# A threshold search with fewer passes, its secant steps on other engines, and logits computed in pairs of row groups

## The chip, the cores and the metric

The kernel runs on one core of one Trainium2 chip. The metric is the device time of one execution in microseconds (us), from the first to the last instruction of that core. Times quoted are medians of several executions. A profile is one more execution, taken by the hardware profiler. Below, PE is TensorE (PEld its weight loads), DVE is VectorE, ACT is ScalarE, POOL is GpSimd. The granted clock is the share of its full speed that the profile gives for PE.

## The reference, cut to what matters

```python
# x: (3327, 256); adj: (3327, 3327), some 0.24% of its entries and the diagonal not zero
h = relu(layernorm(x))
Xf = Xa = h
for n in range(2):                                  # "step 0" and "step 1" below
    q = Xa @ W1.T @ W2.T                            # (3327, 64)
    k = Xa @ W3.T
    p = softmax(q @ k.T)                            # 3327 x 3327
    # nucleus: a row's largest probabilities, kept while the sum of those before is < 0.9
    idx = argsort(-p); sp = p sorted; cs = cumsum(sp)
    mask = scatter(cs - sp < 0.9)
    A = p * mask; A = A / A.sum(-1)
    Xf = R @ Xf                                     # R: (adj + identity), rows normalised
    Xa = A @ Xa
    Z = Z + Xf @ U1[n].T + Xa @ U2[n].T
x = x + layernorm(h + Z)
out = x + relu(adj_norm @ relu(layernorm(x)) @ W.T + b)   # "the final product" below
```

The kernel doesn't sort 3327 probabilities a row. For each row it looks for a threshold on the exponentials `e` that has some 12 to 14 entries fewer above it than the true cut. It then finds the cut among the few largest entries below the threshold. A row that this misses would be found by a test at the end of the program, which takes a slow exact branch.

## The kernel before

The rows go through in 26 blocks of 128, first all of step 0, then all of step 1, then the final product. A block is cut into some hundred pieces. Each piece has a place, a time in us relative to the block's window pass. The program issues all pieces of all blocks in the order of place plus 30 us times the block's number, so several blocks overlap. The numbers set the order in which an engine takes its pieces, and only that: each engine works in order, and waits where its inputs are late.

```python
PERIOD = 30.0
PLACES = (dict(lda0=-85.27, ..., ev1r=-27.94, ev1s=-26.31, st1=-25.42, ..., few=-18.62,   # cut
               st2a=-14.35, ..., st2=-8.7, ..., win=0, ..., drop=20.87, ...),
          dict(xtq_t=-67.29, ..., st2=-16.38, nt2=-16.32, ev3=-15.89, gv1=-12.86, st3=-9.5,  # cut
               nt3=-4.48, ..., win=0, ..., drop=6.98, ...))
```

The search. `e` is 128 x 3327. A pass of ACT sums `relu(t - e)` or `sign(t - e)` over it. The mass pass of DVE sums the entries above `t`. Everything else acts on columns of 128 x 1:

```python
def fma(name, src, scale, bias, f=AF.Identity):        # one column, on ACT
    dst = col(name)
    nc.scalar.activation(dst, src, f, bias=bias, scale=scale)
    return dst

def eval_pass(s, f, name):                             # 3.07 us on ACT
    # ... (junk: a tile that nobody reads)
    nc.scalar.activation(junk, s["e"][:, :N], f, bias=s["t"], scale=-1.0, accum_out=s[name])

def not_few(s):                                        # step 0, on POOL
    nc.gpsimd.tensor_scalar(few, s["sign"], N - 2 * FEW, FAR, op0=ALU.is_lt, op1=ALU.mult)
    nc.gpsimd.tensor_tensor(few, few, s["u"], op=ALU.subtract)
    set_thr(s)

def secant(s, goal):                                   # step 1, on POOL
    t, kc, d = s["t"], s["kc"], s["up"]
    nc.gpsimd.tensor_scalar(num, d, -1.0, d, op0=ALU.mult, op1=ALU.max)
    nc.gpsimd.tensor_scalar(num, t, kc, num, op0=ALU.mult, op1=ALU.add)
    nc.gpsimd.tensor_tensor(slope, s["excess"], s["before"], op=ALU.subtract)
    # ... seven more of this kind, with one pow(den, -1)

def eval_mass(s):                                      # step 1, 3.68 us on DVE
    nc.vector.scalar_tensor_tensor(junk, ev, s["t"], ev, op0=ALU.is_gt, op1=ALU.mult, accum_out=s["mass"])

def drop_rest(i, step, s):                             # "the drop pass", 3.68 us on DVE, once a block
    nc.vector.scalar_tensor_tensor(
        ev, s.pop("w")[:, :N], kept8[:, step * NB + i, 0:1], ev, op0=ALU.is_gt, op1=ALU.mult, accum_out=den)
```

Step 0 evaluates a sum and a count at each of two thresholds, four passes of ACT. Step 1 does the same, then a secant step on POOL, a mass pass on DVE, and a second secant step on POOL.

The logits. Keys lie in two halves of 64 partitions each, so each matmul uses half of the array's rows:

```python
LOGIT_CHUNKS = []                                      # eight chunks, up to 512 columns of one half each
for _c in range(0, HC, 512):
    for _h in range(2):
        _w = min(512, (HC if _h == 0 else N - HC) - _c)
        LOGIT_CHUNKS.append((_h, _c, _w, _h * HC + _c))

def logit_chunk(s, kt, n):                             # eight separate pieces of a block
    half, c0, w, at = LOGIT_CHUNKS[n]
    s["l", n] = pl = ps_l.tile([P, 512], F32, tag="psl", name="p_l")
    rows = slice(half * DA, (half + 1) * DA)
    nc.tensor.matmul(pl[:, :w], s["q"][rows, :], kt[rows, c0 : c0 + w], start=True, stop=True)

def exp_chunk(s, n):                                   # eight exponentials, each with its sum
    nc.scalar.activation(
        s["e"][:, at : at + w], s.pop(("l", n))[:, :w], AF.Exp, accum_out=s["zp"][:, n : n + 1])
```

The product with `R` adds each block's own rows on DVE (piece `prop`) before ACT scales them. POOL issues the gathers: 16 a block in step 0 (eight rows of `adj`, eight of `h`), eight in step 1.

Of the kernel before, what the change touches and what calls it, by code (L numbers as in the profile page):

```python
# [17 lines left out]
P = 128  # L18
# [15 lines left out]
LOGIT_CHUNKS = []  # L34
for _c in range(0, HC, 512):
    for _h in range(2):
        _w = min(512, (HC if _h == 0 else N - HC) - _c)
        LOGIT_CHUNKS.append((_h, _c, _w, _h * HC + _c))
# [37 lines left out]
AIM = (14.0, 12.0)  # L76


QUANT = 1.2815516
DENS = (0.1754983, 0.1595439)  # L80
# [5 lines left out]
FEW = 20.5  # L86
FAR = 60.0
# [18 lines left out]
        lda0=-85.27, flag0=-72.55, lda1=-69.11, xtq_t=-69, lda2=-67.9, xtq_c=-66.8,  # L106
        flag1=-63.82, lda3=-62.27, q1_m=-59.1, flag2=-58.44, q1_c=-56.97, q2_m=-53.29,
        q2_c=-50.53, lg0=-49.96, ex0=-49.75, flag3=-47.66, lg7=-47.53, lg6=-45.4,
        ex7=-44.92, lg4=-44.85, ex6=-44.23, listA=-42.72, lg3=-40.26, ex4=-39.87,
        listN=-39.78, before=-39.78, lg2=-39.65, lg1=-39.48, beforec=-39.06, ex3=-38.97,  # L110
        lg5=-38.89, ex2=-38.69, ex1=-38.26, owners=-36.57, ex5=-36.04, shared=-34.28,
        guess=-33.47, lentc=-33.42, which=-30.52, ev1r=-27.94, ev1s=-26.31, st1=-25.42,
        rows=-21.78, ev2s=-20.12, few=-18.62, ev2r=-15.77, st2a=-14.35, idx=-9.35,
        gv5=-8.72, st2=-8.7, ga0=-5.98, gv3=-4.27, gv7=-1.49, gv4=-1.09, gv1=-0.73,
        win=0, wm0=2.18, wm1=3.73, wm2=6.42, ga5=7.09, gv6=7.44, wm3=9.54, gv0=9.6,
        ga1=9.71, diag=9.75, ga4=10.48, sort=13.78, cut=15.85, ga7=17.26, match=19.36,
        drop=20.87, tr0=21.98, atc0=23.34, tr1=24.39, atc1=25.24, tr2=25.35, att0=25.73,
        tr3=26.42, att1=26.62, atc2=26.87, ga2=27.32, atc3=28.01, tr4=28.07, ga6=29.35,
        gv2=29.61, ga3=30.18, att2=32.01, atc4=32.29, att3=33.26, tr6=34.12, atc6=34.36,
        tr5=35.01, inv=36.42, att4=37.74, atc5=38.12, adj0=38.16, att5=38.64, att6=39.87,  # L120
        attend=39.94, adj1=41.04, stxa=41.5, adj2=42.64, adj3=43.47, adj4=43.71,
        xtk_t=44.19, adj5=44.33, adj6=44.34, xtk_c=44.73, store=45.09, adj7=45.44,
        adj8=48.38, k_m=49.7, k_c=50.09, degA=51.5, prop=52.89, deg=55.98, scale=70.99,
        stxf=84.28,
    ),
    dict(
        xtq_t=-67.29, xtq_c=-62.17, q1_m=-62.02, q1_c=-61.59, q2_m=-58.75, q2_c=-56.62,
        lg0=-55.22, lg4=-54.87, ex0=-52.74, lg3=-51.08, ex4=-50.37, lg7=-48.98, ex3=-47.8,
        lg2=-47.44, ex7=-46.65, lg5=-46.01, ex2=-45.98, ex5=-43.9, lg1=-43.28, lg6=-42.45,
        ex1=-41.17, ex6=-40.83, guess=-38.51, ev1r=-32.26, ev1s=-31.87, st1=-27.61,  # L130
        gv6=-25.6, ev2r=-25.53, ev2s=-24.8, st2a=-24.23, gv7=-21.66, st2=-16.38,
        nt2=-16.32, ev3=-15.89, gv1=-12.86, st3=-9.5, nt3=-4.48, gv5=-4.32, gv0=-1.63,
        win=0, wm0=0.03, wm1=0.86, ld2=0.92, wm2=0.99, wm3=3.29, gv2=4.09, sort=5.17,
        cut=5.26, lda=6.33, match=6.43, drop=6.98, gv4=9.13, gv3=12.4, inv=16.86,
        tr1=18.26, tr0=20.4, atc1=21.2, tf1=21.53, tr2=21.87, tf1c=22.32, adj0=22.42,
        atc0=23.35, atc2=23.87, adj1=24.05, adj2=24.85, adj3=25.18, att0=25.2, adj4=26.4,
        adj5=26.46, tr3=26.7, att1=27.9, adj6=27.96, tr5=28.47, att2=28.91, atc3=29.97,
        adj7=31.68, tr4=32.86, adj8=33.13, atc5=33.42, atc4=33.61, tr6=33.66, prop=33.84,
        att3=33.9, att4=34.32, atc6=34.75, scale=35.17, att5=36.88, mix0=36.94, att6=36.95,
        tf2=38.31, mix1=38.9, attend=39.79, tf2c=40.97, ta2=41.25, ldx=42.46, ta2c=44.29,  # L140
        mix2=47.26, mix3=49.69, resid=50.09, root1=51.53, input2=52.12, root2=80.43,
        node2=81.03, stn=91.32,
# [21 lines left out]
def tile_kernel(ctx: ExitStack, tc: tile.TileContext, x, adj_t, w1t, w2t, w3t, u1t, u2t, ln_g, ln_b, wt, bias, out):  # L164
# [8 lines left out]
    ps_l = ctx.enter_context(tc.tile_pool(name="ps_l", bufs=3, space=bass.MemoryType.PSUM))  # L173
# [3 lines left out]
    ps_m = ctx.enter_context(tc.tile_pool(name="ps_m", bufs=1, space=bass.MemoryType.PSUM))  # L177
# [70 lines left out]

    values = [LN_EPS, 1e-9, 1e-6, -1.0, DOWN, -DOWN, FAR - 2 * DOWN, -0.5 * N, AIM[0] - 0.5 * N]
    values += [-float(np.log(N * d)) for d in DENS]  # L250
# [134 lines left out]
    def list_chunk(i, c, s):  # L385

        if c == 0:
            s["most"] = small.tile([P, NB], F32, name="most", bufs=2)
        b0, nb = ADJ_CHUNKS[c]
        nc.vector.tensor_reduce(  # L390
            s["most"][:, b0 : b0 + nb], s["chunk"].pop(c)[:, :nb, :], AX.X, ALU.max, apply_absolute_value=True
        )
# [21 lines left out]
    def list_before(s):  # L414
        s["p"] = before = ps_m.tile([P, 512], F32, tag="psm", name="p_before")
        nc.tensor.matmul(before[:, 0:1], tri, s["count"], start=True, stop=True)
# [12 lines left out]
    def list_shared(s):  # L429

        s["p"] = p_sh = ps_m.tile([P, 512], F32, tag="psm", name="p_shared")
        w = OVER + 2
        for k in range(SHARED):
            nc.tensor.matmul(
                p_sh[:, k * w : (k + 1) * w], s["own"][:, k * P : (k + 1) * P], s["nodes"][:, SHARED + REG :],
                start=True, stop=True,
            )
# [65 lines left out]
    def adj_gathered(s, k, width, own, acc=adj_acc):  # L503


        if k == 0:
            s["acc"] = acc()
        rows = own if k == SLOTS else s["vg"].pop(k)
        nc.tensor.matmul(  # L509
            s["acc"][:, :width], s["ac"][:, k, :], rows[:, :width], start=(k == 0), stop=(k == SLOTS)  # L510
        )
# [4 lines left out]
    def turn(s, src, space=(ps_m, "psm")):  # L516
# [20 lines left out]
    def key(s, xt, space=(ps_m, "psm")):  # L537
        s["p"] = pk = space[0].tile([P, 512], F32, tag=space[1], name="p_k")
# [23 lines left out]
    def centre(kt, key_sum):  # L562
# [3 lines left out]
        pm = ps_m.tile([P, 512], F32, tag="psm", name="p_mean")  # L566
# [5 lines left out]
    def query_1(s):  # L572
        s["p"] = pq1 = ps_m.tile([P, 512], F32, tag="psm", name="p_q1")
# [7 lines left out]
    def query_2(s):  # L581
        s["p"] = pq = ps_m.tile([P, 512], F32, tag="psm", name="p_q")
# [6 lines left out]
    def logit_chunk(s, kt, n):  # L589
        half, c0, w, at = LOGIT_CHUNKS[n]  # L590
        s["l", n] = pl = ps_l.tile([P, 512], F32, tag="psl", name="p_l")
        rows = slice(half * DA, (half + 1) * DA)
        nc.tensor.matmul(pl[:, :w], s["q"][rows, :], kt[rows, c0 : c0 + w], start=True, stop=True)  # L593

    def exp_chunk(s, n):

        half, c0, w, at = LOGIT_CHUNKS[n]
        if n == 0:
            s["e"] = big.tile([P, N + FILL], F32, tag="e", name="e", bufs=3)
            s["zp"] = small.tile([P, NZ], F32, name="zp")  # L600
        nc.scalar.activation(  # L601
            s["e"][:, at : at + w], s.pop(("l", n))[:, :w], AF.Exp, accum_out=s["zp"][:, n : n + 1]
# [14 lines left out]
    def first_guess(s, step):  # L617

        s["z"] = col("z")
        junk = small.tile([P, NZ], F32, name="junk_z", bufs=1)  # L620
# [7 lines left out]
        ln_c = fma("ln_c", ln_z, -1.0, value[-float(np.log(N * DENS[step]))])  # L628
        s["c"] = fma("c", ln_v, 0.5, ln_c, AF.Exp)

# [6 lines left out]
    def excess(s, aim=0.0):  # L637

        below = fma("below_n", s["sign"], -0.5, value[aim - 0.5 * N])
        rest = fma("rest", s["z"], 1.0 - TOP_P, s["over"])  # L640
        s["before"], s["excess"] = s.get("excess"), fma("excess", below, s["t"], rest)

    def density_step(s):

        s["up"] = fma("up", s["excess"], s["c"], value[DOWN], AF.Relu)

    def step_1(s):
        excess(s)
        density_step(s)
        s["u"] = fma("u1", s["up"], 1.0, s["u"])  # L650
        s["t"] = fma("t1", s["u"], 1.0, value[-DOWN], AF.Exp)

    def mark_few(s):
        s["few"] = few = col("few")
        nc.gpsimd.tensor_scalar(few, s["sign"], N - 2 * FEW, FAR, op0=ALU.is_ge, op1=ALU.mult)

    def not_few(s):
        s["few"] = few = col("few")
        nc.gpsimd.tensor_scalar(few, s["sign"], N - 2 * FEW, FAR, op0=ALU.is_lt, op1=ALU.mult)
        nc.gpsimd.tensor_tensor(few, few, s["u"], op=ALU.subtract)  # L660
        set_thr(s)
# [4 lines left out]

    def step_2(s):

        s["u"] = fma("u2", s["up"], -1.0, s["few"], AF.Relu)
        s["t"] = fma("t2", s["u"], -1.0, value[FAR - 2 * DOWN], AF.Exp)  # L670

    def secant(s, goal):

        num, den, slope, up, u = (col(n) for n in ("num", "den", "slope", "up_s", "u_s"))
        t, kc, d = s["t"], s["kc"], s["up"]
        nc.gpsimd.tensor_scalar(num, d, -1.0, d, op0=ALU.mult, op1=ALU.max)  # L676
        nc.gpsimd.tensor_scalar(num, t, kc, num, op0=ALU.mult, op1=ALU.add)
# [662 lines left out]
```

## Time and profile before

| | before |
|---|---|
| median of 3 runs | 2070.38 us (2068.54 to 2074.57) |
| span of the profiled execution | 2153.0 us, mean granted PE clock 0.919 |
| a block of step 0 / of step 1, by the stretches in the prediction | 29.25 / 35.5 us |
| ACT passes of 3.07 us a block, step 0 / step 1 | 4 / 4 (and one mass pass on DVE in step 1) |

The profile's page gives the chain of work that ended last, by engine, and below that its costliest groups of instructions. A row of a group has line, engine, operation, the tiles written and read, their shapes and the count; then busy us and mean ns; then idle time just ahead of it and what ended it. Of the kernel before:

```profile
PE 38%; ACT 34%; POOL 16%; issue 8%; DVE 2%; DMA 1%; another core or an unknown queue 1%; POOLq 0%; SPq 0%; ACTq 0%; DVEq 0%
...
L593 PE MATMUL p_l<-kt,q 64*128 64x512 f32 (+2 forms) x832 | 347.0, 602 | 29.5 <-ACT e L601 16.3
...
L701 DVE SCALAR_TENSOR_TENSOR w<-e,t 128x3327 f32<-128x3327 f32 x26 | 95.8, 3684 | 128.8 <-ACT t L614 128.8
```

POOL has 16% of the chain though it does little but one-column arithmetic and the issuing of gathers. The last row is step 1's mass pass: DVE stands idle for 128.8 us in front of 26 of them. The logits take 347.0 us of PE, 6.7 a block. How the rest of the profile reads is in the prediction.

### The profile page before, as it was taken

The page shows a single profiled execution, that of the slowest core. Times are in us where ns is not written, and L with a number is a line of the kernel's source. Part 1 is how long each engine was busy: PE and PEld are TensorE (multiplying, and loading weights), DVE is VectorE, ACT ScalarE, POOL GpSimd, SP SyncE. Part 2 cuts the span into 40 slices and gives each one's busy share as a digit, 9 for nine tenths or more (in the row PEclk, how much of TensorE's full clock was granted, in tenths as well). Part 3 has the DMA queues.
Part 4 walks back from the last instruction along what each step waited for, and adds up shares of the span by engine and source line. Part 5 has one row for each costly group of instructions (what it writes and reads, how often), then busy time and mean ns, then how long its engine had stood idle before and what let it go on. Part 6 is the DMA issues. An engine that isn't in the chain of part 4 may idle for free.

```text
span 2153.0 us, 27658 instructions
## 1 busy us (share of the span) xinstructions
PE 1845.7 (86%) x8114; PEld 1338.9 (62%) x8114; DVE 1491.8 (69%) x3713; ACT 1506.6 (70%) x3547; POOL 1414.8 (66%) x1733
## 2 busy tenths in 40 slices
PE   6589999999999997568989898989998988568886
PEld 4266666666666666346666676666666666456664
DVE  6678999998999995177878777878787878200001
ACT  5879999998999994677878787878787874100000
POOL 0467777787777776277676767676767676256552
PEclk9599999999999999579999999999999999789887
DMA  7334454454454432311222221212121212366652
GB/s 221 92 114 136 148 152 134 139 151 140 144 152 132 144 110 79 123 40 57 68 63 66 59 71 59 70 54 75 55 74 57 73 53 71 127 203 204 207 184 84
DMA packets 115472, 236.11 MB, mean 110 GB/s; under 512 B 22003, under 2 KB 70256, under 8 KB 114544
## 3 DMA queue, kind: packets, MB, share of 16 engines
q1 hardware_dynamic: 78240, 143.04, 20.6%
q0 software_dynamic: 34304, 89.29, 15.0%
q10 hardware_dynamic: 2768, 1.93, 0.3%
q8 instruction: 66, 1.08, 0.2%
q14 instruction: 94, 0.77, 0.1%
HBM read 198.38 MB, written 35.79 MB: 109 GB/s over the span
## 4 chain that ended last, share of the span: by engine, by line
PE 38%; ACT 34%; POOL 16%; issue 8%; DVE 2%; DMA 1%; another core or an unknown queue 1%; POOLq 0%; SPq 0%; ACTq 0%; DVEq 0%
ACT ja L635 19%; PE att_acc L804 10%; PE p_l L593 7%; PE adj_acc L509 5%; PE late_acc L1107 4%; PE late_acc L509 4%; ACT at L793 4%; POOL num L676 3%; PE p_t L785 3%; POOL vg L499 3%; ACT e L601 2%; POOL den L681 1%; ACT t L614 1%; PE p_turn L520 1%; PE p_o L899 1%
## 5 line engine op out<-in xcount | busy, mean ns | idle before, releaser
L635 ACT ACTIVATE ja<-e,t 128x3327 uint8<-128x3327 f32 x208 | 639.7, 3075 | 0.1
L499 POOL DMA_INDIRECT vg<-xf_hbm,v_idx x208 | 382.3, 1838 | 95.5 <-issue 55.3
L593 PE MATMUL p_l<-kt,q 64*128 64x512 f32 (+2 forms) x832 | 347.0, 602 | 29.5 <-ACT e L601 16.3
L804 PE MATMUL att_acc<-h,at 128*128 128x256 f32 (+1 forms) x1352 | 326.1, 389 | 25.6 <-issue 10.2
L804 PE MATMUL att_acc<-xa,at 128*128 128x256 f32 (+1 forms) x1352 | 320.7, 382 | 0.0
L499 POOL DMA_INDIRECT vg<-h_hbm,v_idx x208 | 271.6, 1306 | 59.6 <-issue 45.5
L481 POOL DMA_INDIRECT ac<-in_adj_t,a_idx x208 | 267.6, 1286 | 60.3 <-issue 53.3
L804 PEld LDWEIGHTS att_acc<-h,at 128*128 128x128 f32 (+1 forms) x1352 | 249.2, 192 | 71.4 <-ACT u L614 11.2
L804 PEld LDWEIGHTS att_acc<-xa,at 128*128 128x128 f32 (+1 forms) x1352 | 250.0, 191 | 47.5 <-issue 17.4
L601 ACT ACTIVATE e<-p_l 128x512 f32<-128x512 f32 (+2 forms) x416 | 211.4, 511 | 70.1 <-PE p_l L593 69.2
L499 POOL DMA_INDIRECT vg<-hn_hbm,v_idx x160 | 152.1, 950 | 145.3 <-DMA hn_hbm<-hn 45.2
L785 PE MATMUL p_t<-ident,e 128*128 128x128 f32 x1352 | 223.3, 295 | 27.8 <-ACT at L793 19.5
L727 DVE MAX8 cand<-w 128x8 f32<-128x208 f32 x832 | 238.7, 360 | 1.0
L793 ACT COPY at<-p_t 128x512 f32<-128x512 f32 (+1 forms) x364 | 188.8, 542 | 62.0 <-PE p_t L785 39.5
L509 PE MATMUL adj_acc<-vg,ac 128*128 128x257 f32 (+1 forms) x832 | 232.2, 393 | 0.0
L785 PEld LDWEIGHTS p_t<-ident,e 128*128 128x128 f32 x1352 | 171.7, 153 | 90.7 <-ACT at L793 33.7
L593 PEld LDWEIGHTS p_l<-kt,q 64*128 64x128 f32 x832 | 129.6, 204 | 146.9 <-issue 102.0
L720 DVE SCALAR_TENSOR_TENSOR w<-e,t 128x3327 f32<-128x3327 f32 x52 | 191.3, 3678 | 25.4 <-ACT t L614 25.2
L769 DVE SCALAR_TENSOR_TENSOR e<-w,kept,e 128x3327 f32<-128x3327 f32 x52 | 191.6, 3685 | 1.8
L765 DVE MATCH_REPLACE8 w<-kept,e 128x3335 f32<-128x3335 f32 x52 | 188.1, 3617 | 0.0
L910 DVE TENSOR_TENSOR o<-p_o,b_l 128x256 f32<-128x256 f32 x26 | 11.0, 425 | 254.7 <-remote 91.1
L701 DVE SCALAR_TENSOR_TENSOR w<-e,t 128x3327 f32<-128x3327 f32 x26 | 95.8, 3684 | 128.8 <-ACT t L614 128.8
(410 smaller groups left out, 2856.1 us busy)
## 6 DMA issues: line engine op xcount, KB each, us to landing
adj_sb<-in_adj_t SPq DMA_DIRECT2D x78, 448.0 KB
ac<-ac_hbm SPq DMA_DIRECT2D x46, 576.0 KB
ac_hbm<-ac SPq DMA_DIRECT2D x26, 576.0 KB
adj_row<-in_adj_t SPq DMA_DIRECT2D x6, 1664.0 KB
adj_sb<-in_adj_t SPq DMA_DIRECT2D x26, 320.0 KB
h_hbm<-h SPq DMA_DIRECT2D x26, 128.5 KB
vg<-h_hbm,v_idx POOLq DMA_INDIRECT x208
ac<-in_adj_t,a_idx POOLq DMA_INDIRECT x208
```

The lines of the kernel that those rows point to most:

```text
L481: nc.gpsimd.indirect_dma_start(s["ac"][:, k, :], None, adj_rows, bass.IndirectOffsetOnAxis(ap=s["a_idx"][:, k : k + 1], axis=0))
L499: nc.gpsimd.indirect_dma_start(t[:, :width], None, hbm[:, :], bass.IndirectOffsetOnAxis(ap=v_idx[:, i, k : k + 1], axis=0))
L509: nc.tensor.matmul(s["acc"][:, :width], s["ac"][:, k, :], rows[:, :width], start=(k == 0), stop=(k == SLOTS))
L593: nc.tensor.matmul(pl[:, :w], s["q"][rows, :], kt[rows, c0 : c0 + w], start=True, stop=True)
L601: nc.scalar.activation(s["e"][:, at : at + w], s.pop(("l", n))[:, :w], AF.Exp, accum_out=s["zp"][:, n : n + 1])
L635: nc.scalar.activation(junk, s["e"][:, :N], f, bias=s["t"], scale=-1.0, accum_out=s[name])
L720: nc.vector.scalar_tensor_tensor(w[:, :N], ev, s["t"], ev, op0=ALU.is_le, op1=ALU.mult, accum_out=s["below"])
L727: nc.vector.max(s["cand"][:, 8 * n : 8 * n + 8], s["w"][:, c0 : c0 + cw])
L769: nc.vector.scalar_tensor_tensor(ev, s.pop("w")[:, :N], kept8[:, step * NB + i, 0:1], ev, op0=ALU.is_gt, op1=ALU.mult, accum_out=den)
L785: nc.tensor.transpose(pt[:kb, c : c + P], s["e"][:, b * P : b * P + kb], ident)
L793: nc.scalar.copy(at[:, :full], pt[:, :full])
L804: nc.tensor.matmul(s["att"][:, :D], at[:kb, c : c + P], v[b][:kb, :D], start=(b == 0), stop=(b == NB - 1))
```

## The change

Its intent is to make the search cheaper. After a first sum and count, later thresholds are judged by counts alone: the missing mass between two thresholds is taken as the difference of the counts times a value between them. Step 0 loses one ACT pass, step 1 loses DVE's mass pass. Step 0's last step is computed on ACT, step 1's two secant steps on DVE; POOL only prepares for them, and in step 0 that is eight operations where there were three. Two logit matmuls of different row groups are issued back to back into a tile of two PSUM banks, and one exponential takes both. An identity matmul adds a block's own rows in the product with `R`. The last of four flag chunks goes from DVE to ACT. Pieces are placed anew in both steps.

```diff
-LOGIT_CHUNKS = [...eight, by half...]
+LOGIT_CHUNKS = [(c, min(LOGIT_W, HC - c)) for c in range(0, HC, LOGIT_W)]
 ...                                      # PLACES: every number is new, in both steps
-        (step 0) ev1r=-27.94, ev1s=-26.31, st1=-25.42, ev2s=-20.12, few=-18.62, ev2r=-15.77, st2a=-14.35, st2=-8.7,
+        (step 0) ev1s=-17.4, ev1r=-13.7, st1=-10.2, ev2s=-9.9, aux=-3.2, st2=-1.1,
-        (step 1) ev2r=-25.53, ev2s=-24.8, st2a=-24.23, st2=-16.38, nt2=-16.32, ev3=-15.89, st3=-9.5, nt3=-4.48,
+        (step 1) aux=-20.1, ev2s=-19.8, sec1=-16.4, nt2=-15.3, ev3s=-14.2, aux2=-13.7, sec2=-12.1, nt3=-4.7,
 ...
-    ps_l = tile_pool(name="ps_l", bufs=3, space=PSUM)
+    ps_l = tile_pool(name="ps_l", bufs=2, space=PSUM)        # two-bank tiles
-    ps_m = tile_pool(name="ps_m", bufs=1, space=PSUM)        # its users share ps_t's two banks
 ...
+        if c == len(ADJ_CHUNKS) - 1:                         # list_chunk: the last flags
+            for b in range(nb):
+                nc.scalar.activation(junk, a[:, b, :], AF.Abs, accum_out=s["most"][:, b0 + b : b0 + b + 1])
+            return
 ...
+        weights = s["ac"][:, k, :] if k < TERMS else ident   # adj_gathered: one term more
 ...
     def logit_chunk(s, kt, n):
-        half, c0, w, at = LOGIT_CHUNKS[n]
-        nc.tensor.matmul(pl[:, :w], s["q"][rows, :], kt[rows, c0 : c0 + w], start=True, stop=True)
+        c0, w = LOGIT_CHUNKS[n]
+        s["l", n] = pl = ps_l.tile([P, 2 * LOGIT_W], F32, tag="psl", name="p_l")
+        for half in range(2):
+            rows = slice(half * DA, (half + 1) * DA)
+            at = half * LOGIT_W
+            nc.tensor.matmul(pl[:, at : at + w], s["q"][rows, :], kt[rows, c0 : c0 + w], start=True, stop=True)
 ...
+    def prepare_2(s, step):                                  # piece aux, on POOL
+        set_thr(s)
+        go = col("go")
+        nc.gpsimd.tensor_scalar(go, s["up"], -DOWN, None, op0=ALU.add)
+        size = pool_fma("size", go, -1.0, go, ALU.max)
+        if step == 0:
+            # ... prior, num, mid, goal, uf: five more
+        else:
+            # ... kc, num, u1, uh1: four more
 ...
+    def step_2(s):                                           # step 0, on ACT
+        ln_n = fma("ln_n", s["num"], 1.0, 0.0, AF.Ln)
+        # ... eleven more
+    def secant(s, goal, last):                               # step 1, on DVE
+        nc.vector.tensor_sub(more, sign, sign0)
+        nc.vector.scalar_tensor_tensor(size, more, -1.0, more, op0=ALU.mult, op1=ALU.max)
+        nc.vector.tensor_scalar(den, size, 0.5, PSEUDO, op0=ALU.mult, op1=ALU.add)
+        nc.vector.reciprocal(den, den)
+        # ... four or five more
-    def eval_mass(s): ...
```

Also, the final product's accumulators rotate over four banks for three.

## The prediction

> **What bounds the kernel now.** I read first the busy shares by stretch of time, cut where the chain of waits changes its repeating lines; columns: stretch, its length, busy us and instructions of PE, PEld, DVE, ACT, POOL, then clock, DMA share, GB/s. The first line is the heart of step 0 (20 row blocks), the second step 1 (25 blocks), the third the final product.
>
> ```profile
> 184.00:769.00 585.00, 564.28 (x2623) 397.99 (x2622) 539.96 (x1499) 553.29 (x1311) 450.48 (x481) 1.00 0.48 144
> 892.00:1780.00 888.00, 774.54 (x3358) 561.02 (x3359) 677.49 (x1454) 690.71 (x1591) 634.10 (x869) 0.92 0.20 61
> ...
> 1870.00:2153.00 283.00, 212.01 (x830) 164.50 (x830) 22.24 (x53) 20.26 (x52) 150.19 (x159) 0.84 0.57 186
> ```
>
> Step 0 takes 585/20 = 29.25 us a block, with PE 28.2, ACT 27.7 and DVE 27.0 busy: nearly full. Step 1 takes 888/25 = 35.5, with PE 31.0, ACT 27.6, DVE 27.1: nobody full, so a chain of waits sets it. The other 530 us of the 2153 (start, turn between steps, final product) I call the rest. The waits of step 1, longest first (total us, times, longest):
>
> ```profile
> POOL few L655 <- ACT ja L635: 149.4, 25, 28.8
> DVE w L701 <- ACT t L614: 124.6, 25, 37.2
> ACT t L614 <- POOL u_s L685: 119.1, 50, 5.0
> ```
>
> Once a block DVE waits 5.0 us for a threshold and ACT twice 2.4 us for the secant step on POOL. The instructions in order of time show the ring (start, duration; POOL first, then DVE):
>
> ```profile
> 1400.94 3.65 POOL L692 TENSOR_SCALAR up<-up 128x1 f32<-128x1 f32 x1
> ...
> 1408.83 4.55 POOL L499 DMA_INDIRECT vg<-xf_hbm,v_idx  x1 [0.50 <-issue]
> ```
> ```profile
> 1400.83 3.68 DVE L769 SCALAR_TENSOR_TENSOR e<-w,kept,e 128x3327 f32<-128x3327 f32 x1
> ...
> 1408.69 3.68 DVE L701 SCALAR_TENSOR_TENSOR w<-e,t 128x3327 f32<-128x3327 f32 x1 [4.17 <-ACT t L614]
> ```
>
> A one-column POOL operation takes 3.65 us because it starts beside DVE's two-input pass and ends with it; a gather behind the mass pass takes 4.55. The ring: DVE from the window pass to the drop, without a break, 21.8 (1382.7 to 1404.5); first secant on POOL 3.8; threshold on ACT 0.4; mass pass on DVE 3.7; held gather 1.1; second secant 5.1; threshold 0.3: 36.2 us, one block of step 1.
>
> **What the Trainium skill says.** "SBUF — State Buffer", Who interferes with whom: a DVE instruction with two SBUF inputs contends with a GpSimd instruction that reads SBUF, and the second to start fully blocks. The trace agrees: 3.65 and 4.55 us above, against 0.22 to 0.3 for such operations and 0.95 for such gathers elsewhere. "TensorE: Matmul & The Clock Gate", Part 3: matmuls in different row groups run together. The trace agrees: one logit chunk (x2) and two chunks of different halves (x4) take the same time:
>
> ```profile
> 466.32 1.12 PE L593 MATMUL p_l<-kt,q 64*128 64x512 f32 x2
> 467.38 0.38 PE L416 MATMUL p_before<-count,tri 128*128 128x1 f32 x2
> 467.69 1.13 PE L593 MATMUL p_l<-kt,q 64*128 64x512 f32 x4
> ```
>
> "ScalarE: Activation LUTs", What ACT_TABLE_LOAD costs: a fixed start plus 0.833 ns an element, back-to-back ones overlapping by about 93 ns. The trace has 591 ns for 512 columns and 256 for 128, some 0.87 ns a column. So I sum by start-to-start times.
>
> **The change part by part, per block.** The fixed order of pieces was also printed from the built program; it gives order, no times.
>
> *Step 1, the ring.* Both secants move to DVE (8 and 9 one-column operations at 0.14 to 0.20 us, about 1.7 and 1.9 with gaps) and the mass pass is gone; a count on ACT replaces the sum-and-count pair's second half, so ACT keeps four 3.06 us passes. POOL only prepares (9 operations, 3 us, plus 8 gathers), away from the path most of the time. What is left is engine sums:
> - DVE: 27.1 - 3.8 (mass pass) - 0.4 (prop) - 0.15 (max) + 3.6 (secants) = 26.4.
> - ACT: 27.6 - 0.3 (eight exps become three of 1024 columns at about 1.02, one of 254 at 0.35, one of 1 at 0.2: 3.6 for 3.9) + 0.1 (small operations) = 27.4.
> - PE: logits before 5.8 (1.9 for two of one half, 1.27, 2.2, 0.42); paired 3 x 1.06 + 0.45 = 3.6; the new identity matmul, two passes of 0.215, +0.43. 31.0 - 2.2 + 0.4 = 29.2. That the 31.0 is work and not stretched by waiting I checked against step 0: its 28.2, less keys and lists (1.2), plus 16 mixing passes at 0.215 (3.4) and two more turns (0.8), gives 31.2.
>
> Step 0 shows how close an order of pieces comes to its fullest engine: 29.25 over 28.2, 1.05 more. 29.2 + 1.0 = **30.2 us for 35.5**, over 25 intervals -132.
>
> *Step 0, where I expect no gain.* PE: logits 5.9 to 3.6, identity +0.43: 28.2 to 26.4. DVE: last flag chunk -0.8, prop -0.42, degree -0.3, max -0.13: 25.4. ACT: one pass less -3.06; exps -0.3; step 2 of the search from 1.8 to 3.3 (12 dependent columns at 0.2 to 0.42) +1.5; five flag sums 128x128 with their read-accumulators +1.35; two more degree functions and order +0.35: 27.5. But POOL is fuller than its busy share:
>
> ```profile
> L499 POOL DMA_INDIRECT vg<-h_hbm,v_idx x161 | 214.2, 1331 | 45.6 <-issue 34.5 <-POOL v_idx L474 5.4 <-PE p_t L785 3.7
> L481 POOL DMA_INDIRECT ac<-in_adj_t,a_idx x160 | 206.6, 1291 | 46.7 <-issue 40.5 <-PE p_l L593 3.3
> ...
> L659 POOL TENSOR_SCALAR few<-sign 128x1 f32<-128x1 f32 x20 | 5.1, 257 | 32.9 <-ACT ja L635 22.1 <-issue 10.9
> ```
>
> The 0.28 us ahead of every gather (45.6/161) is a gap of issuing, the same before nearly each; only the 32.9 us ahead of "few" is waiting. (585 - 33)/20 = 27.6 us a block taken. The three operations few, few, thr (1.0 us) become eight (thr, go, size, prior, num, mid, goal, uf) at 0.30 to 0.40 start to start: 2.7. 27.6 + 1.7 = 29.3, and the eight can't start before the first step on ACT is done: +0.5. **29.8 for 29.25**, over 25 intervals +14. The relief of PE, DVE and ACT lies beside POOL.
>
> *The rest.* One search without POOL's arithmetic in filling step 1: -5. The final product, whose accumulators now rotate over four banks for three, waits for gathers and rows (DMA share 0.57): 0.
>
> Sum: 2153 + 14 - 132 - 5 = 2030 profiled. The timed median over the profiled span is 2070.38/2153 = 0.9616, taken to hold: 2030 x 0.9616 = 1952, say **1950 us**, 5.8% less.
>
> **Rivals.** *A new wait for the old in step 1:* DVE runs in order, so a secant can stand behind sort or match while ACT waits; and the transposes, queries and turns share two banks where they had three, logits two double tiles. For: ACT's count, DVE's secant, ACT's next count form a ring within one block. Against: between count and threshold ACT has two exps, two copies (3.2 us) to do, and DVE has cut, node and match (some 6) between its secants, longer than one ACT pass plus threshold (3.7). If it held, 33 for 30.2: +70 profiled, 2018 timed. *Step 0 does gain:* if POOL's locks fall elsewhere (its gathers average 1.31 against a free 0.95, some 5.7 us a block lost), ACT at 27.5 plus 0.8 would set 28.3: -37, 1915. *POOL gets worse:* late eight operations hold ACT's second step, which holds the window: 31.5, +42, 1992. *The slow exact branch* behind the final test would be taken if the new search missed a window; the time would be several times longer. Nothing in the profile speaks for it; under 1%.
>
> **Range and chances.** Step 0 at 28.3 to 31 and step 1 at 29 to 32, with 15 either way for the rest, rarely all together: 1890 to 2010. Not being 2% faster (over 2029) needs step 1 above 33.5: 5%; slower almost only by the slow branch: 1%.
>
> **What would show it.** Step 1: the waits "DVE w <- ACT t" for a mass pass and "ACT t <- POOL u_s" are gone, block distance 29 to 32, PE busiest, its clock above 0.92. Step 0: distance about 29.8, the idle time ahead of POOL's preparations near zero or made of waits for ACT's "up", while PE falls to about 26.5 and DVE to 25.5 busy. Logit chunks x4 take 1.1 us. If step 0 is under 29, my POOL sum is wrong; if step 1 is over 32, look for ACT waiting on "u_s" of DVE, or PE on the two transpose banks. The timed ratio differing from 0.9616 would shift all.

## The result, and the profile after

The kernel after takes 1902.23 us, the median of four runs (1899.71 to 1904.4). The kernel before takes 2070.43 in the same rounds. The ratio is 0.9185, with a 95% interval of 0.9167 to 0.9203. Here and below, a ratio is the mean time of one kernel's fast runs over the mean of the other's fast runs of the same rounds, so it isn't quite the ratio of the quoted medians. The outputs are right, and the slow branch isn't taken. The profiled execution spans 1900.6 us at a mean granted clock of 0.953.

First the busy time by stretch, with the same columns as in the prediction: 20 blocks of step 0, 21 of step 1, the final product.

```profile
186.00:800.00 614.00, 543.28 (x2698) 404.25 (x2699) 526.56 (x1402) 564.25 (x1532) 506.59 (x587) 0.97 0.47 139
1000.00:1600.00 600.00, 594.83 (x3067) 461.56 (x3066) 559.74 (x1576) 578.97 (x1298) 338.01 (x382) 1.00 0.26 82
1678.00:1900.00 222.00, 188.03 (x830) 155.42 (x830) 22.32 (x53) 19.38 (x52) 150.98 (x159) 0.93 0.73 237
```

Step 1 now has PE busy for 594.83 of 600 us: it is the bound, at 27.8 of the 28.0 us that a block takes. Its granted clock is 1.00, where it was 0.92 (0.95 in 20 whole blocks, from 1005.15 to 1723.30). In step 0 no engine is as full. ACT, the fullest, has 92%.

The chain of work that ended last and two groups of the page, for the same readings as before:

```profile
PE 27%; ACT 13%; DVE 10%; DMA 3%; issue 1%; POOL 0%; SPq 0%; DVEq 0%; POOLq 0%; ACTq 0%
...
L588 PE MATMUL p_l<-kt,q 64*128 64x512 f32 (+1 forms) x832 | 202.3, 588 | 40.0 <-ACT e L608 26.3
...
L676 POOL TENSOR_SCALAR go<-up 128x1 f32<-128x1 f32 x52 | 87.1, 1674 | 125.7 <-ACT up L621 125.7
```

The logits went from 347.0 to 202.3 us of PE for the same 832 matmuls. POOL has left this chain, which can be read only as far as it goes: it names one path back from the end. The group `go` shows a one-column operation with a mean of 1674 ns, far above the 0.22 us that it takes alone.

The longest waits of step 1, and below them a stretch of DVE there in order of time (start, duration, then as above, with the wait in brackets):

```profile
POOL go L676 <- ACT up L621: 123.1, 26, 9.8
POOL size L665 <- DVE go_s L719: 64.2, 26, 3.5
POOL num L665 <- ACT t_inv L621: 54.4, 40, 2.3
DVE more L713 <- ACT ja L644: 48.3, 26, 25.1
```

```profile
1410.28 0.16 DVE L713 TENSOR_TENSOR more<-sign 128x1 f32<-128x1 f32 x1 [0.38 <-ACT ja L644]
...
1411.76 0.19 DVE L725 TENSOR_TENSOR u_s<-u,go_s 128x1 f32<-128x1 f32 x1
...
1414.35 3.62 DVE L798 MATCH_REPLACE8 w<-kept,e 128x3335 f32<-128x3335 f32 x1
1417.88 0.15 DVE L713 TENSOR_TENSOR more<-sign 128x1 f32<-128x1 f32 x1
...
1419.27 0.22 DVE L723 SCALAR_TENSOR_TENSOR u_s<-u_s,go_s,few 128x1 f32<-128x1 f32 x1
1419.40 3.68 DVE L802 SCALAR_TENSOR_TENSOR e<-w,kept,e 128x3327 f32<-128x3327 f32 x1
```

The waits left in step 1 are POOL's, which isn't on the path, and one of DVE for a count (of its 48.3 us, 25.1 are a single wait at the start of the step). The secant steps take 1.7 and 1.6 us from first start to last end. The first stands ahead of the cut, the second fits between the match and the drop pass, and DVE goes on without a break.

In step 0, POOL in order of time:

```profile
403.17 0.25 POOL L670 TENSOR_SCALAR thr<-z 128x1 f32<-128x1 f32 x1
403.39 3.56 POOL L676 TENSOR_SCALAR go<-up 128x1 f32<-128x1 f32 x1
...
411.77 4.14 POOL L490 DMA_INDIRECT vg<-h_hbm,v_idx  x1 [0.30 <-issue]
...
430.63 0.29 POOL L462 TENSOR_SCALAR a_idx<-a_row 128x8 int32<-128x8 f32 x1 [0.42 <-DVE a_row L455]
...
433.90 0.25 POOL L670 TENSOR_SCALAR thr<-z 128x1 f32<-128x1 f32 x1
```

From `thr` to `thr` it is 30.7 us, one block. In it POOL waits for another engine for 0.42 us. All else is its own operations and gaps of issuing of about 0.3 us. The other blocks are alike: from 189.62 to 767.54, 19 blocks, the only wait of POOL for another engine longer than such a gap is this one. The `go` at 403.39 ends with the drop pass of DVE (403.18 to 406.86), and the gather at 411.77 lies beside DVE's window pass (411.41 to 415.09). So POOL is the bound of step 0, and its busy share of 83% hides that.

To compare runs, the start of the drop pass is read from each trace. It happens once a block, so the differences give a block's time. "Start" is the time up to the first drop pass, "turn" the time from the last of step 0 to the first of step 1, "end" the time from the last one to the end. Three numbered chips appear. Chips 11 and 12 run the kernel before at a median of 2068.2 and 2069.2 us, chip 2 at 2175.8.

| trace | chip | span | step 0, mean (median) | step 1, mean | start | turn | end |
|---|---|---|---|---|---|---|---|
| before, first profile | not numbered | 2153.0 | 29.56 (29.40) | 35.80 | 101.4 | 94.7 | 322.9 |
| after, first profile | not numbered | 1900.6 | 30.24 (30.33) | 28.01 | 97.3 | 86.9 | 260.0 |
| before, again | 2 | 2196.3 | 30.57 (29.39) | 35.72 | 101.2 | 95.1 | 342.9 |
| before, again | 12 | 2064.9 | 28.97 (29.38) | 35.52 | 101.4 | 92.1 | 259.1 |
| after, again | 12 | 1898.7 | 30.17 (30.30) | 27.98 | 97.9 | 87.9 | 259.2 |

On chip 12 the change takes 166.2 us off the span. That is 25 x 7.54 = 188.5 less in step 1, 25 x 1.20 = 30.0 more in step 0, 3.5 and 4.2 less at the start and the turn, and nothing in the end.

### The profile page after: what moved, and what is told of

Same layout as the page of the kernel before. It is cut to its first block, busy times and chain, and to the rows that moved or that the text cites. A ratio compares the mean times of both kernels' runs of the same rounds, so it can differ in the third digit from the quotient of the medians.

```text
span 1900.6 us, 28030 instructions
## 1 busy us (share of the span) xinstructions
PE 1663.2 (88%) x8218; PEld 1273.6 (67%) x8218; DVE 1411.8 (74%) x3922; ACT 1484.6 (78%) x3703; POOL 1214.3 (64%) x1421
## 4 chain that ended last, share of the span: by engine, by line
PE 27%; ACT 13%; DVE 10%; DMA 3%; issue 1%; POOL 0%; SPq 0%; DVEq 0%; POOLq 0%; ACTq 0%
PE att_acc L836 8%; ACT ja L644 7%; PE late_acc L1153 4%; PE late_acc L503 3%; PE adj_acc L503 3%; DVE w L798 3%; DVE e L802 3%; DMA vg<-hn_hbm,v_idx 3%; PE p_t L817 2%; PE p_l L588 2%; ACT at L825 2%; PE p_z L907 1%; PE p_o L945 1%; PE p_turn L512 1%; ACT e L608 1%
## 5 line engine op out<-in xcount | busy, mean ns | idle before, releaser
L644 ACT ACTIVATE ja<-e,t 128x3327 uint8<-128x3327 f32 x182 | 558.4, 3068 | 1.2
L490 POOL DMA_INDIRECT vg<-xf_hbm,v_idx x208 | 333.9, 1605 | 87.0 <-issue 36.0
L836 PEld LDWEIGHTS att_acc<-h,at 128*128 128x128 f32 (+1 forms) x1352 | 263.0, 197 | 39.8
L817 PE MATMUL p_t<-ident,e 128*128 128x128 f32 x1352 | 210.0, 282 | 77.5 <-ACT at L825 48.7
L472 POOL DMA_INDIRECT ac<-in_adj_t,a_idx x208 | 206.6, 993 | 60.3 <-issue 60.0
L588 PE MATMUL p_l<-kt,q 64*128 64x512 f32 (+1 forms) x832 | 202.3, 588 | 40.0 <-ACT e L608 26.3
L753 DVE SCALAR_TENSOR_TENSOR w<-e,t 128x3327 f32<-128x3327 f32 x52 | 191.6, 3685 | 35.2 <-ACT t L621 32.7
L608 ACT ACTIVATE e<-p_l 128x1024 f32<-128x1024 f32 x208 | 180.2, 866 | 18.2 <-PE p_l L588 14.3
L503 PEld LDWEIGHTS adj_acc<-vg,ac 128*128 128x128 f32 x832 | 142.0, 192 | 56.1 <-issue 33.2
L676 POOL TENSOR_SCALAR go<-up 128x1 f32<-128x1 f32 x52 | 87.1, 1674 | 125.7 <-ACT up L621 125.7
```

Of the source, the lines that this page charges most:

```text
L472: nc.gpsimd.indirect_dma_start(s["ac"][:, k, :], None, adj_rows, bass.IndirectOffsetOnAxis(ap=s["a_idx"][:, k : k + 1], axis=0))
L490: nc.gpsimd.indirect_dma_start(t[:, :width], None, hbm[:, :], bass.IndirectOffsetOnAxis(ap=v_idx[:, i, k : k + 1], axis=0))
L503: nc.tensor.matmul(s["acc"][:, :width], weights, rows[:, :width], start=(k == 0), stop=(k == last))
L588: nc.tensor.matmul(pl[:, at : at + w], s["q"][rows, :], kt[rows, c0 : c0 + w], start=True, stop=True)
L608: nc.scalar.activation(halves(s["e"])[:, :, c0 : c0 + w], logits_of(pl)[:, :, :w], AF.Exp, accum_out=s["zp"][:, n : n + 1])
L817: nc.tensor.transpose(pt[:kb, c : c + P], s["e"][:, b * P : b * P + kb], ident)
```

## The experiments

Twelve kernels ran. All gave right results. My theory at the outset was the prediction's: step 1 is freed from a ring of waits through POOL's secants and is left with PE's sum, and step 0 is bound by POOL. The rivals were that POOL's secants or the mass pass alone made the ring, that the pairs of logits do little, and that the loss in step 0 comes from something other than POOL's eight operations.

### The kernel before, unchanged, on chip 2 and on chip 12

No edit. The question is what the factor 0.9616 of the prediction, timed over profiled, stands for.

> The kernel before, unchanged, to see whether its profiled span of 2153 us (4% above its timed 2070) is typical. If profiling costs this kernel 4%, this run's span is again about 2150 and 0.96 was a property of it that the kernel after does not share. If the first profile was an odd execution, the span here is about 2069, and the stage that is shorter than in the first profile (I expect the final product, 283 us there) is the one that was odd; then the step-0 and step-1 block distances 29.25 and 35.5 stay.

> The kernel before on the chip of after_again, to compare stages of the two on one chip: step 1 35.7 for 28.0, step 0 29.4 to 30.6 for 30.3, and from the last drop of step 1 to the end within 15 us of each other. If the four accumulators of the final product matter, after_again's end is 20 us or more shorter.

Measured: 2198.17 us on chip 2 and 2066.65 us on chip 12, against medians of 2175.84 and 2069.2 of the timed runs on the same chips, 1.0% more and 0.1% less. The final product by stretch, from the last drop pass of step 1 on: first the kernel before on chip 2, then the same on chip 12.

```profile
1854.00:2196.00 342.00, 248.10 (x952) 190.90 (x952) 36.00 (x91) 27.96 (x73) 151.63 (x160) 0.81 0.50 159
```
```profile
1806.00:2064.00 258.00, 210.85 (x952) 174.34 (x952) 36.43 (x91) 26.74 (x73) 151.66 (x160) 0.92 0.65 210
```

The same 952 matmuls and 160 POOL instructions take 342 us on one chip and 258 on the other, at 159 GB/s for 210. So the profiler costs nothing that shows, and the factor compared two executions of different speed. Of the 88.1 us between the first profile of before and the one on chip 12, 63.8 are in the end. 15 more are in step 0, where single blocks are longer while the median is the same. Why chip 2 is slower there isn't settled.

### The kernel after, unchanged, on chip 12

> The kernel after, unchanged, as the reference of this chip. The chip of the first set ran the kernel before at 2176 where another ran it at 2070, so ratios count. I expect the ratio to before at 0.92 to 0.93, step 0 at 30.3 and step 1 at 28.0 to 28.5 between drops, and on a slow chip the difference in the final product.

Measured: 1902.04 us, ratio 0.9205 (0.9184 to 0.9226). The trace repeats the first one within 0.1 us a block. It is the base for what follows.

### The preparing operations of step 0 moved from POOL to DVE, in two places

```diff
-        aux=-3.2          (step 0)
+        aux=-6.05         (aux_on_dve: just ahead of the drop pass)
+        aux=-5.5          (aux_after_drop: just behind it)
     def prepare_2(s, step):
+        if step == 0:
+            # the same eight operations, thr, go, size, prior, num, mid, goal, uf, on nc.vector
+            return
         set_thr(s)
```

> The kernel after, with the eight preparing operations of step 0 on VectorE (placed just ahead of the drop pass) in place of POOL. If POOL's list of work sets step 0 at 30.7 us a block, POOL falls to about 27, and the distance falls to 28.7 to 29.3 with ACT (28.2 busy) fullest: 26 x 1.6 = 40 us, 1862. If ACT, or the two shared transpose banks, set 30.7, nothing moves: 1902, or it gets worse by VectorE's 1.5 us a block.

> As aux_on_dve (the eight preparing operations of step 0 on VectorE), but placed after the drop pass, where ACT's up has been there for 5 us, so VectorE does not wait as it did there (36 us in 18 blocks). If POOL sets step 0 in the kernel after, and aux_on_dve only put a wait of VectorE in its place, the distance falls to 28.8 to 29.5, 20 to 40 us under after_again. If the list chain (codes, before, owners, shared, which, rows) with its gathers sets step 0, it stays at 30.3 and POOL only waits more for 'which'.

The first ran on chip 2: 2017.22 us, ratio 0.9284 (0.9212 to 0.9356) to before there. No unchanged kernel after was on that chip. Its step 0 has 31.34 us a block, and DVE now stands still ahead of the drop pass for ACT's `up` (29.5 us in 15 times, within 560 us). It is inconclusive.

The second ran on chip 12: 1873.57 us, ratio 0.9065 (0.9046 to 0.9084), against 1902.04 of the kernel after. That is 28.5 us less. Step 0 falls from 30.17 to 29.30 us a block, step 1 stays at 27.99. 19 blocks of its step 0 by stretch, and two of the longest waits there:

```profile
226.00:786.00 560.00, 509.08 (x2523) 384.77 (x2521) 503.36 (x1470) 527.48 (x1430) 415.29 (x396) 0.96 0.49 141
```
```profile
PEld p_t L821 <- ACT at L829: 49.4, 25, 2.6
POOL a_idx L462 <- DVE a_row L455: 47.9, 19, 2.7
```

POOL now waits 2.5 us a block for DVE's list of rows (47.9 us in 19 times). Before this edit it waited 0.42 us in the block shown. It has 21.7 us of 29.3 busy, and ACT, with 27.6, is next. Taking the eight operations away from POOL, 5.7 us with their lock in the block shown further up (403.17 to 408.87), made step 0 shorter by 0.9 us a block. So POOL set its time, and the eight operations beside the drop pass were part of it. That 5.7 us taken away gain only 0.9 has two parts. The `ac` gathers, 0.99 us each in the kernel after, take 1.28 here (193.1 us in 151), 2.3 more for a block's eight: where `go` stood beside the drop pass, a gather now does (389.61 to 392.95, the drop pass 388.45 to 392.13). And the wait for the list takes 2.5. The one-column operations cost DVE little: the eight start within 0.83 us behind the drop pass. This version is the fastest.

### The secant steps of the kernel before moved from POOL to DVE, in two places

```diff
     def secant(s, goal):                  # before
-        nc.gpsimd.tensor_scalar(num, d, -1.0, d, op0=ALU.mult, op1=ALU.max)
-        # ... nine more on gpsimd, pow(den, -1) among them
+        nc.vector.scalar_tensor_tensor(num, d, -1.0, d, op0=ALU.mult, op1=ALU.max)
+        # ... nine more on vector, reciprocal(den) for the pow; so too in secant_2 and secant_3
-        st3=-9.5
+        st3=-15.5                         # before_secant_early only: right behind the mass pass
```

> The kernel before, with the two secants of step 1 on VectorE and all else as it was, the mass pass too. If the ring through POOL was the cause, the block distance of step 1 falls from 35.5 to 31 to 32 (PE with its 31 fullest) and the time by 90 to 110 us, to 1960 to 1980. If the mass pass itself is what costs (rival), the distance stays at 34 or more: over 2030.

> As before_secant_dve, with one place changed: the second secant directly behind the mass pass on VectorE, ahead of the residual that waits for TensorE. before_secant_dve stayed at 35.3 because the secants went into VectorE's own line behind that wait: busy 31.5 of 35.2. If that is the reason, step 1 falls to 31.7 to 32.5 here and the time by 70 to 90 us against before. If something else holds 35 (PE and its exps), it stays within 1 us.

Measured: the first takes 2171.95 us on chip 2, ratio 1.0018 (0.9919 to 1.0117), with 35.35 us a block in step 1 (35.72 before, on that chip). The second takes 2047.96 us on chip 12, ratio 0.9905 (0.9886 to 0.9924), with 34.86 (35.52 before). Both miss what I expected, 31 to 32.5. Step 1 of the second by stretch (21 blocks):

```profile
1000.00:1740.00 740.00, 677.55 (x3007) 497.62 (x3006) 671.19 (x1861) 598.44 (x1371) 230.01 (x172) 0.96 0.23 66
```

DVE has 671.19 us busy in 740, 31.6 of 34.9 a block, and of the rest 1.4 is a wait of `prop` for PE, 0.4 one for the threshold. PE is busy for 32.0 of 35.1 (20 whole blocks). So POOL's slow columns by themselves aren't what holds step 1 of the kernel before. Whoever computes them, a chain with both the mass pass and two secant steps in it fills one line of work. Moved to DVE, that line is DVE's own.

### The kernel after with the mass pass put back

```diff
+        ev3m=-14.15                       # step 1, behind the second count
+            do["ev3m"] = lambda: eval_mass(s)     # its sum is not used
```

> The kernel after, with the mass pass of before put back into step 1 as an extra pass of VectorE (3.7 us, its sum unused), between the cut and the match. In the kernel after, TensorE is busy 99% of step 1 (27.8 of 28.0 a block) and VectorE 26.2. If VectorE's line was what held step 1 at 35 when only the secants moved, this fills it to 30.0 and the distance grows to 30.5 to 32, +60 to +100 us against the kernel after, which is about 0.95 to 0.97 of before on a fast chip. If VectorE has the room, under 28.8.

Measured on chip 11: 2021.64 us, ratio 0.9759 (0.9737 to 0.9781). Step 1 has 32.70 us a block, 4.7 more than the kernel after, for a pass of 3.7 and above the 30.5 to 32 expected; step 0 is unchanged (30.16). Step 1 by stretch, and the first wait of PE:

```profile
1000.00:1600.00 600.00, 545.13 (x2610) 412.66 (x2609) 541.66 (x1371) 503.83 (x1102) 352.15 (x325) 0.93 0.24 70
```
```profile
PEld p_t L824 <- DVE e L758: 52.7, 18, 2.9
```

PE waits 2.9 us a block for the drop pass, its clock is 0.93 again, and PE and DVE are both at 90%. Here the pass is 3.7 us on DVE and costs 4.7. Of all single parts tried, the mass pass is the largest.

Not all of the 4.7 is waiting. In 20 whole blocks, PE's 144 matmul instructions a block take 30.0 us here and 28.0 in the kernel after. The traces show where: PE stands idle for 2.73 us up to 1211.85; from 1213 to 1216 its granted clock is 0.50, and the four logit matmuls that start at 1213.64 take 2.08 us, where four such take 1.13 at 1218.70. The kernel before on chip 12 has the same after a wait of 2.02 us up to 1208.67 (0.50 from 1210 to 1212), yet not after one of 2.20 us up to 1244.46. So a wait of PE can cost twice here, once in idle time and once in slower matmuls; why only some do isn't tested.

### The kernel after with the secant steps on POOL

```diff
     def secant(s, goal, last):            # after
-        nc.vector.tensor_sub(more, sign, sign0)
-        # ... the rest on vector
+        nc.gpsimd.tensor_tensor(more, sign, sign0, op=ALU.subtract)
+        # ... the rest on gpsimd, pow(den, -1) for the reciprocal
```

> The kernel after, with both secants of step 1 on POOL again (8 and 10 operations at 0.3 us), all else the same. If the move off POOL matters by itself, step 1 grows from 28.0 to 30.5 to 33 a block, the second secant being held by the drop pass. If only the mass pass and the order mattered, it stays under 28.8, since POOL is half idle in step 1.

Measured on chip 11: 1943.28 us, ratio 0.939 (0.9364 to 0.9416). Step 1 has 29.66 us a block, 1.7 more. That is neither of the two ranges named. The waits of step 1:

```profile
DVE w L753 <- ACT t L621: 75.7, 21, 3.6
POOL more L714 <- ACT ja L644: 67.8, 41, 2.2
...
ACT t L621 <- POOL u_s L725: 37.0, 21, 1.8
```

With POOL in the ring, DVE waits 3.6 us a block for the threshold of its window pass (75.7 in 21 times), where the kernel after doesn't wait. The place of the secants matters, then, but only once the mass pass is out: 1.7 us there, 0.4 and 0.7 with it in (35.72 to 35.35 on chip 2, 35.52 to 34.86 on chip 12).

### The kernel after with the pairs of logits undone

```diff
-        do[f"lg{n}"] = lambda n=n: logit_chunk(s, kt, n)
+        do[f"lg{n}"] = lambda n=n: logit_chunk(s, kt, n, 0)
+        do[f"lh{n}"] = lambda n=n: logit_chunk(s, kt, n, 1)     # other matmuls in between
```

(The places of the second halves lie 0.1 to 2.4 behind the first ones, with other matmuls between; two exponentials move by 0.2 to let them pass.)

> The kernel after, with the two halves of each logit tile issued apart, another matmul between them, so that no two row groups run together; exps and tiles the same. If pairing is what lets PE keep up in step 1 (26.6 busy of 28.1), step 1 grows to 29.3 to 30 a block, and step 0, set by POOL, stays at 30.7: 1930 to 1950. If PE has slack in both, the time stays within 10 us of 1902. If PE sets step 0 too, 1960 and more.

Measured on chip 2: 2191.97 us, ratio 1.0083 (1.0006 to 1.016) to before on the same chip. On balance the whole gain is gone on this chip. Step 1 has 31.54 us a block and step 0 35.08. Against the chip-2 run with the preparing operations on DVE (28.35 in step 1), step 1 is 3.2 longer, and against the kernel after on chip 12 it is 3.6. Logit matmuls of the kernel after in step 1, then of this one:

```profile
1400.45 1.13 PE L588 MATMUL p_l<-kt,q 64*128 64x512 f32 x4
```
```profile
1400.64 1.12 PE L590 MATMUL p_l<-kt,q 64*128 64x512 f32 x2
1404.01 1.12 PE L590 MATMUL p_l<-kt,q 64*128 64x512 f32 x2
```

Four matmuls of both row groups take as long as two of one. Three full chunks come to 3 x 1.12 = 3.4 us a block saved, and step 1, with PE 99.7% busy (718.10 of 720 us), is longer by about that. In 20 whole blocks the logits take 7.2 us of PE a block for 3.6, and PE has no idle time at all. I had expected 1.3 to 2 more, and step 0 to stay at 30.7. Step 0 is 4.9 longer than that of the kernel after on chip 12, more than the matmuls' own 3.4. I haven't taken that apart, and the chip may be in it: the kernel before has 30.57 us a block there, for 28.97 on chip 12.

### The last flag chunk back on DVE, and then also the identity matmul undone

Both start from the fastest version, the preparing operations behind the drop pass.

```diff
-        if c == len(ADJ_CHUNKS) - 1: ... five Abs sums on nc.scalar      # aux_flag_dve
-        adj9=48,                                                          # aux_flag_prop: this as well
+        prop=48,                       # step 1's own rows added on DVE
```

> aux_after_drop with the fourth flag chunk back on VectorE (0.8 us there for five activations of 0.41 on ACT). In aux_after_drop step 0 is 29.3 a block with ACT 27.6 busy. If ACT sets it now, 28.3 to 28.8; if PE and ACT's copies in turn (two transpose banks), 29.0 to 29.3. Step 1 stays at 28.0.

> aux_flag_dve, and in step 1 the identity matmul undone: the row's own term is added on VectorE as before. If TensorE sets step 1 at 27.8 of 28.0, taking 0.43 away gives 27.6 to 27.8, 5 to 10 us under aux_flag_dve. If a ring through ACT and VectorE sets it, no change or longer, since VectorE then waits for the sum ahead of its drop pass.

Measured on chip 11, where the kernel before has 2068.21: 1898.93 us for the first, ratio 0.917 (0.9151 to 0.9189), and 1957.58 for the second, ratio 0.9461 (0.9439 to 0.9483). The version they start from had 0.9065, so the first is worse by about 25 us (22 by the ratios). Its step 0 has 30.35 us a block for 29.30, outside both ranges expected. ACT is relieved (477.52 us busy in 560, for 527.48), yet the block is longer. The waits of its step 0:

```profile
POOL a_idx L456 <- DVE a_row L449: 58.8, 18, 3.4
DVE crowd L409 <- ACT nodes L404: 44.5, 19, 2.6
...
ACT ln_n L615 <- DVE num L676: 41.1, 18, 2.5
```

DVE passes its delay on to POOL's indices and to ACT's step. So in this arrangement the flags on ACT are worth about 1 us a block of step 0, although ACT is the busiest engine there.

The second differs from the first in step 1: 30.39 us a block for 28.00. The longest wait on ACT there, and the turn behind it:

```profile
ACT xf L872 <- DVE prop L856: 48.3, 19, 2.8
PEld p_turn L509 <- ACT xf L872: 42.2, 19, 2.6
```

The identity matmul costs PE, the bound, about 0.5 us a block (the product with `R` takes 5.0 us of PE in the kernel before and 5.5 in the kernel after). Undoing it costs 2.4: the own rows then go from PE to DVE to ACT and back to PE, and PE waits 2.2 us a block for them. I had expected a small gain. The place that I gave the addition on DVE may not be its best, so 2.4 is what this arrangement costs.

## Why the prediction was right, and where its sizes were off

The prediction said 1950 us, between 1890 and 2010, faster. Measured: 1902, near the lower end. By its steps:

- **Step 1's ring goes, and PE's sum is left.** Right. The waits "DVE w <- ACT t" for a mass pass and "ACT t <- POOL u_s" are gone, PE has 99% and a clock of 1.00. The rival of a new wait in their place didn't come, as DVE had both secants done in time. One reading of the ring was off: DVE's line isn't "without a break", it has 0.89 us of idle time ahead of `prop` at 1391.85.
- **Step 1's size: 30.2 predicted, 28.0 measured.** The step that was mis-sized is PE's sum with its slack, 29.2 + 1.0, which measured 27.8 + 0.2. The sum started from a wrong 31.0. The stretch from 892 to 1780 begins 43 us before the first drop pass of step 1 (935.19), and it holds the transposes of 22.7 blocks (591, 26 a block) and the mixing of 23, but its busy time was divided by 25. In 20 whole blocks, from drop pass to drop pass, the same trace has 32.2 us of PE a block, and the kernel after 28.0:

  | PE busy us a block, 20 whole blocks | logits | mixing (p_z) | transposes (p_t) | product with `R` | attention, turns, queries | all |
  |---|---|---|---|---|---|---|
  | before, 1005.15 to 1723.30 | 6.2 | 5.1 | 4.8 | 5.0 | 15.1 | 32.2 |
  | after, 998.00 to 1559.95 | 3.6 | 4.1 | 4.0 | 5.5 | 14.9 | 28.0 |
  | after with the mass pass, 1009.00 to 1670.81 | 4.3 | 4.8 | 4.6 | 5.5 | 14.9 | 30.0 |

  Groups overlap in time, so each row's groups come to some 4 us more than its last column; the differences between rows nearly add up.

  The pairs save 2.6 (2.2 predicted) and the identity costs 0.5 (0.4 predicted). The other 1.9, mixing and transposes, wasn't work that stays: the prediction took all of PE's busy time for work. The last row shows that it comes back with a wait. There the mixing matmuls with `xt_f` take 458 ns each, with no idle time just ahead of them and a clock of 0.93, where they take 387 to 390 in the runs that have a clock of 1.00 in step 1 (the kernel after twice, with the secants on POOL, unpaired, and with the preparing operations on DVE on chip 2).

  The prediction's check against step 0 counted 16 mixing passes at 3.4 us, where they take 5.1 before and 4.1 after, and met the wrong 31.0 by chance. So 30.2 was nearer than its terms deserved: the base was too low by 1.2, and 1.9 of it went away unforeseen. DVE and ACT came out at 26.2 and 27.05 for 26.4 and 27.4 predicted, but their bases of 27.1 and 27.6 came from the same stretch (28.2 and 28.1 in whole blocks), so that agreement is partly luck. The slack of 1.0, taken over from step 0 of before, is 0.2: an order of pieces can come closer to its fullest engine than that one did. Step 1 saved 188.5 us where I had 132.
- **What made the ring.** The prediction drew it whole, and named POOL's slow columns twice in it. The experiments show that no single part holds the 7.5 us. With the secants moved alone in the kernel before, 0.4 and 0.7 us were gained; undone from the kernel after, the mass pass costs 4.7, the secants on POOL 1.7, the pairs about 3.6, and the identity matmul, undone from the run with the flags on DVE, 2.4. Their sum, 12.4, exceeds the gain, so they aren't parts that add: in each trace another wait or engine comes last (PE's wait for the drop pass, DVE's for the threshold, PE's own 99.7%, PE's wait for the turn). No run puts the mass pass and POOL's secants back together, which would be the ring itself, so that it alone made the 35.5 isn't shown.
- **Step 0 gets a little worse with POOL as the bound.** Right in kind: POOL works without waiting, and the version with those operations on DVE takes 0.9 us off a block. The size was 29.8 and is 30.3 (median), by terms that partly cancel. The sum for the eight operations, 2.7 us, left out the lock: with `go` beside the drop pass they take 5.7, from 403.17 to 408.87. The eight `ac` gathers of a block, on which part of that lock seems to have lain, fall from 1.29 to 0.99 us each, 2.4 less, which the prediction named only in a rival. The 0.5 for a late start didn't come (`go` has 0.0 us of idle time ahead of it in 19 blocks). The rival "step 0 gains" fails, and "POOL gets worse" (31.5) was too far. This cost 30.0 us on the same chip where I had 14.
- **The final product unchanged.** Right: 259.1 and 259.2 us on the same chip.
- **The factor 0.9616.** Wrong as a mechanism. It stood for two executions of different speed, mostly in the final product, and not for a cost of profiling. The profiled run of the kernel after has 1902.61 us, as its timed ones. The factor did little harm: against the span of before on chip 12, the same sum gives 2065 - 123 = 1942 us.
- **ACT's 0.87 ns a column.** It rests on a mean of 256 ns for 128 columns in step 0 alone. Over the whole trace that mean is 267, which gives 0.84.

So the mechanism held: step 1 is left with PE's sum and step 0 with POOL's line. What was mis-sized is step 1's PE sum with its slack, and so the time saved, 168 us where 120 was forecast.

What stays open: whether the mass pass and POOL's secants together are the whole ring, why PE's clock falls after some waits and not after others, why chip 2 needs 84 us more for the final product, how the 4.9 us of unpaired logits in step 0 come about, and whether the identity matmul is worth 2.4 us against a better place of the addition.

## What to carry to other kernels

When a step's time lies above every engine's busy time, sum the engines, but over whole blocks, and don't take busy time for work: here a stretch with 23 blocks of products was divided by 25, and of PE's true 32.2 us a block 1.9 went away with the waits. An engine's busy share isn't its load. POOL with 83% was the bound of step 0, and moving eight tiny operations from beside a two-input pass of DVE to DVE itself gained 1.5%. When a chain of several parts is broken, undo each part alone from the finished version, because a part moved alone in the old one (the secants: at most 1%) doesn't show what it is worth in the new one (2%).

## What the Trainium skill lacked or had wrong

- "SBUF — State Buffer", Who interferes with whom, says that a DVE instruction with two SBUF inputs contends with a GpSimd one that reads SBUF. The runs agree (3.56 us for an operation of 0.22). The same page has `tensor_tensor` not stalling a DMA issued by GpSimd, and infers the reason: the generation of descriptors needs the write interface, and `tensor_tensor` takes only the read interface. Here gathers issued by GpSimd beside `scalar_tensor_tensor`, a two-input pass, took 4.14 us (4.55 in the kernel before) for 0.95 elsewhere. The page lacks that an indirect DMA's issue is held beside such a pass. Whether that comes from the reading of its indices, which lie in SBUF, no run here tells.
- No page found gives the gap ahead of each indirect DMA on GpSimd: 0.28 to 0.31 us in nearly every one here, beside 0.95 us of its own. With 16 gathers a block that is an estimated 16 x 1.25 = 20 us of a block's 30.
- "VectorE: DVE Perf Modes", The TRN2 errata (SBUF-src ops pay a fixed extra latency per instruction), has (N + 151)/0.96 ns for an fp32 add of two tensors. For one column that is 158 ns, and the secant's operations have 0.14 to 0.22 us; for 3327 columns it is 3.62 us against 3.68 for the fused passes. It fits well. What it lacks is that dependent one-column operations follow at about 0.2 us from start to start, gap included (eight and nine of them in 1.7 and 1.6 us).
- "GPSIMD Engine Reference", 3.1 Elementwise, in its tables of measured operations has durations at 2048 columns only. One-column operations on GpSimd took mostly 0.19 to 0.38 us, and 0.56 to 0.60 for a `pow`. Ten of them, a secant step, took 5.4 us with a lock of 2.1 in it, against 1.6 for DVE's nine.
